# Node stages of a two-layer graph network taken in steps inside the edge passes, with the passes run from the last destinations down

## The chip, the cores and the metric

One core of one Trainium2 chip runs one program. The metric is the device time in microseconds, the median of several executions; lower is better. A core has five engines with instruction streams of their own: TensorE (PE; its weight loads are listed as PEld), VectorE (DVE), ScalarE (ACT), GpSimd (POOL) and SyncE (SP). Each takes its instructions in order, and they meet at semaphores. DMAs are issued from SP, ACT or POOL.

## The reference

N = 30000 nodes with 128 features, E = 960000 edges sorted by destination. The destinations are 30000 times the square of a uniform number, so low node numbers have more edges. Layer 0 has two relational convolutions with 32 edge types, layer 1 a gated convolution with 4 edge types:

```python
def _rel_graph_conv(h, basis, coeff, bias, src, dst, etype, norm):
    W = jnp.einsum('rb,bdf->rdf', coeff, basis)
    Hr = jnp.einsum('nd,rdf->nrf', h, W)
    msg = Hr[src, etype] * norm
    agg = jax.ops.segment_sum(msg, dst, num_segments=N)
    return agg + bias

h = relu(layernorm(x))
h1 = relu(_rel_graph_conv(h, basis1, coeff1, bias1, ...))
x = x + _rel_graph_conv(h1, basis2, coeff2, bias2, ...)
h = relu(layernorm(x))
for t in range(4):
    k, q, v = h @ Wk[t] + bk[t], h @ Wq[t] + bq[t], h @ Wv[t] + bv[t]
    msg = where(edge_type == t, sigmoid(k[dst] + q[src]) * v[src], 0.0)
    outs.append(segment_sum(msg, dst) + h @ Ws[t] + b[t])
x = x + mean(outs)
```

Every convolution reads rows of arbitrary source nodes, so its input table must be complete before it starts.

## The kernel before, in words

**State.** One tile `agg` [128 features x 30080 nodes] stays in SBUF. Each edge pass adds into its columns; `x` and the biases are added to it between passes.

**Before the passes.** The edge arrays are rewritten to offsets within windows (`prep`, line 153), a flag chooses between the path for well-spread sorted edges (`sorted_path`, line 275) and a general one, and the first layer norm writes table `h0` (line 223).

**Edge passes.** `edge_pass` (line 285) runs 25 iterations (`NI`) of 100 groups (`NG`); a group is three tiles of 128 edges whose destinations lie in one window of 32 nodes. Groups come in twenties of five (`NS` = 20 steps of `S` = 5, index `s`, with `g` the place in the five), and four stages of 25 groups per iteration set how far engines may run apart (`stage_boundary`, `leave_stage`). The order of all instructions in an iteration is written out by hand (`manual_schedule`): each engine keeps the order of the program's text.

- In passes c1 and c2 (`rel_body`, line 325) POOL gathers three times 128 source rows (`hg`, line 107, called at 391), DVE builds `sb` (one-hot destination times eight coefficients, line 395), PE multiplies `hg` by `sb` into `pa` (line 401), ACT copies it to `ab` (line 405), and once per five groups PE multiplies by the eight bases into `po` (line 364, `bases_out`) and DVE adds five windows into `agg` (line 323). Once per five groups SP loads edge types `er` (line 337), DVE makes a one-hot `oh` (line 344), PE turns it into coefficients `pc` (line 347) and DVE scales them to `ce` (line 356).
- In pass g (`gate_body`, line 431 on) POOL gathers q and v rows (`qv`), SP loads windows of the k table (`kw`) and types (`kb`), PE picks k rows into `pk` (line 455, `keys`), DVE adds q, ACT takes the sigmoid, DVE multiplies by v into `msg`, and PE sums by window (line 465, `sums`).
- The indices `idx` of an iteration's gathers, with `relc` and `nrm`, are loaded by SP in four parts (`loads`, line 306), one stage ahead.

**Stages between.** Three stages stand between or behind the passes, each a plain loop over all nodes; no gather runs in them.

- Middle (lines 514 to 535): relu of `agg`, transposed and stored as table `h1`; `x` loaded, transposed, plus bias, as the new `agg`.
- Node (lines 540 to 560): for each of 235 blocks of 128 nodes transpose, layer norm, transpose back, three products with weights of 512 columns (line 261), tables `ktab` and `qvtab` stored from ACT and SP, and the node's own product added to `agg`.
- Final (lines 565 to 576): `agg` transposed and stored to the output.

Of the kernel before, what the change touches and what calls it, by code (L numbers as in the profile page):

```python
# [9 lines left out]
F32 = mybir.dt.float32  # L10
# [8 lines left out]
P = 128  # L19
# [24 lines left out]
NI = NGR // NG  # L44
EPS = 1e-5
# [18 lines left out]
def kernel(  # L64
    ctx: ExitStack,
    tc: tile.TileContext,
    x: bass.AP,
    src: bass.AP,
# [28 lines left out]
    h1 = nc.dram_tensor("h1", (NP, D), F32, kind="Internal").ap()  # L97
    agg1 = nc.dram_tensor("agg1", (NA, D), F32, kind="Internal").ap()
    agg2 = nc.dram_tensor("agg2", (NA, D), F32, kind="Internal").ap()
    ktab = nc.dram_tensor("ktab", (NP * T, D), F32, kind="Internal").ap()  # L100
    qvtab = nc.dram_tensor("qvtab", (NP * T, 2 * D), F32, kind="Internal").ap()
# [35 lines left out]
    for i, (bas, cof) in enumerate(((basis1, coeff1), (basis2, coeff2))):  # L137
        bt = consts.tile([P, B, D], F32, name=f"basis{i}")
        nc.scalar.dma_start(bt, bas.rearrange("b d f -> d b f"))
        ct = consts.tile([P, 4, B], F32, name=f"coeff{i}")  # L140
        nc.vector.memset(ct, 0.0)
        for q in range(4):
            nc.scalar.dma_start(ct[q * R:(q + 1) * R, q, :], cof)
        basis.append(bt)
        coeff.append(ct)
# [7 lines left out]
    with tc.tile_pool(name="prep", bufs=2) as prep, \  # L153
# [42 lines left out]
        nc.vector.tensor_reduce(nbad, bad, AX.XY, ALU.add)  # L196
        pbad = prep_ps.tile([1, 1], F32, name="pbad")
        nc.tensor.matmul(pbad, lhsT=nbad, rhs=ones[:TP], start=True, stop=True)
        nc.vector.tensor_copy(flag, pbad)
    n_bad = nc.values_load(flag[0:1, 0:1], min_val=0, max_val=2 * CH * TP)  # L200

    def normalised(pool, xt, kn, name):

        st = pool.tile([P, kn, 6], F32, name=f"{name}_st")
        mv = pool.tile([P, kn, 2], F32, name=f"{name}_mv")
# [3 lines left out]
        rs = pool.tile([P, kn], F32, name=f"{name}_rs")  # L209
        nc.scalar.activation(rs, mv[:, :, 1], AF.Sqrt, bias=eps)  # L210
        nc.vector.reciprocal(rs, rs)
        hn = pool.tile([P, kn, D], F32, name=f"{name}_hn")
# [62 lines left out]
    def sorted_path():  # L275
        with ExitStack() as all_:
            state = all_.enter_context(tc.tile_pool(name="state", bufs=1))
            agg = state.tile([P, NP], F32, name="agg")
# [6 lines left out]
            def edge_pass(name, body):  # L285
                with tc.tile_pool(name=f"{name}_io", bufs=NQ) as io, \
                        tc.tile_pool(name=f"{name}", bufs=2) as pool, \
                        tc.tile_pool(name=f"{name}_c", bufs=1, space=PSUM) as cps, \
# [4 lines left out]
                    nc.vector.tensor_copy(ic, icol)  # L293
                    with tc.For_i(0, NI, 1, iteration_sync="staggered") as i:
                        with tc.manual_schedule():
                            body(i, io, pool, ps, iw, ic)
# [28 lines left out]
            def rel_body(table, bas, cof):  # L325
                def body(i, io, pool, ps, iw, ic):
# [8 lines left out]
                    def types(s):  # L335
                        er[s] = pool.tile([P, TQ, TP], I32, name="er", bufs=3)
# [5 lines left out]
                    def onehot(s):  # L342
                        oh[s] = pool.tile([P, TQ, TP], F32, name="oh", bufs=3)
                        nc.vector.tensor_scalar(oh[s], er[s], icol4, None, op0=ALU.is_equal)  # L344
                        pc[s] = ps.tile([TP, TQ, 4, B], F32, name="pc")
# [24 lines left out]
                    for s in range(2):  # L370
                        types(s)
                        onehot(s)
                    coefficients(0)
                    for s in range(NS):
# [12 lines left out]
                        for g in range(S):  # L387
                            t0 = (s % SB * S + g) * G
                            hg = pool.tile([TP, G, D], F32, name="hg", bufs=20)
# [3 lines left out]
                            for j in range(G):  # L393
                                sb = pool.tile([TP, B, W], F32, name="sb", bufs=15)
# [11 lines left out]
                            if g == 0 and s + 2 < NS:  # L406
                                onehot(s + 2)
                            if g == 1 and s:
                                bases_out(s - 1)
                            if g == 2 and s + 1 < NS:  # L410
                                coefficients(s + 1)
                            if g == 3 and s > 1:
                                add_windows(po[s - 2], base[(s - 2) // SB], s - 2)
                            if g == 3 and s % SB == 1:
                                base[k] = bases(i, k, DVE)
                    bases_out(NS - 1)
                    for s in (NS - 2, NS - 1):
                        add_windows(po[s], base[NQ - 1], s)
                return body

            def gate_body(i, io, pool, ps, iw, ic):
# [30 lines left out]
                def keys(n):  # L452
                    pk[n] = ps.tile([TP, G, D], F32, name="pk", bufs=5)
# [21 lines left out]
                keys(1)  # L475
                for n in range(NG):
# [17 lines left out]
                    if n + 2 < NG:  # L494
                        keys(n + 2)
# [8 lines left out]
                    if g == 4 and s % SB == 0:  # L504
                        base[k] = bases(i, k, DVE)
                sums(NG - 2)
                sums(NG - 1)
                add_windows(po[NS - 1], base[NQ - 1], NS - 1)


            edge_pass("c1", rel_body(h0, basis[0], coeff[0]))


            MB = 4
            with tc.tile_pool(name="mid", bufs=3) as mid, \
                    tc.tile_pool(name="mid_ps", bufs=2, space=PSUM) as mps:
                for b0 in range(0, NB, MB):
                    m = min(MB, NB - b0)
                    cs = slice(b0 * P, (b0 + m) * P)
                    rows = slice(b0 * P, (b0 + m) * P)  # L520
                    r = mid.tile([P, MB, P], F32, name="r")
                    nc.scalar.activation(r[:, :m].rearrange("p m n -> p (m n)"), agg[:, cs],
                                         AF.Relu, bias=b1c)
                    xt = mid.tile([P, MB, D], F32, name="xt")
                    nc.sync.dma_start(xt[:, :m], x[rows, :].rearrange("(m p) d -> p m d", p=P))
                    pr = mps.tile([P, MB, D], F32, name="pr")
                    px = mps.tile([P, MB, P], F32, name="px")
                    for k in range(m):
                        nc.tensor.transpose(pr[:, k, :], r[:, k, :], ident)
                        nc.tensor.transpose(px[:, k, :], xt[:, k, :], ident)  # L530
                    h = mid.tile([P, MB, D], F32, name="h")
                    nc.vector.tensor_copy(h[:, :m], pr[:, :m])
                    nc.scalar.dma_start(h1[rows, :].rearrange("(m p) d -> p m d", p=P), h[:, :m])
                    nc.vector.tensor_scalar(agg[:, cs], px[:, :m].rearrange("p m n -> p (m n)"),
                                            b2c, None, op0=ALU.add)

            edge_pass("c2", rel_body(h1, basis[1], coeff[1]))


            with tc.tile_pool(name="nodew", bufs=1) as nodew, \  # L540
                    tc.tile_pool(name="node", bufs=3) as node, \
                    tc.tile_pool(name="node_ps", bufs=1, space=PSUM) as nps:
                wall, ball, wsm = node_weights(nodew)
                b4 = nodew.tile([P, T], F32, name="b4")
                nc.scalar.dma_start(b4, bass.AP(tensor=bs.tensor, offset=bs.offset,
                                                ap=[[1, P], [D, T]]))
                bsc = nodew.tile([P, 1], F32, name="bsc")
                nc.vector.tensor_reduce(bsc, b4, AX.X, ALU.add)
                nc.vector.tensor_scalar(bsc, bsc, 1.0 / T, None, op0=ALU.mult)
                for b in range(NB):  # L550
                    cs = slice(b * P, (b + 1) * P)
                    px = nps.tile([P, 1, D], F32, name="px")
                    nc.tensor.transpose(px[:, 0, :], agg[:, cs], ident)
                    hn = normalised(node, px, 1, "node")
# [246 lines left out]
```

## Time and profile before

| | us |
|---|---|
| median of 3 runs | 29649.91 (29645.66 to 29655.3) |
| profiled execution | 29622.14, its span 29620.4 |
| start to the first gather of c1 | 346.4 |
| pass c1, first to last gather | 9383.5 |
| pass c2, first to last gather | 9385.5 |
| pass g, first to last gather | 9414.1 |
| middle, node and final stage, about | 108, 859, 79 |

Mean granted TensorE clock: 0.698 of full speed. The costliest groups of instructions (columns: line, engine, operation, tiles, count, then busy time and mean ns of one, then idle time before them with what ended most of it):

```profile
L107 POOL DMA_INDIRECT hg<-h,idx x15000 | 14178.1, 945 | 5056.4 <-issue 4382.0
L401 PE MATMUL pa<-sb,hg 128*128 128x256 f32 x30000 | 11034.6, 490 | 3480.1 <-DMA hg<-h,idx 1943.2
L395 DVE SCALAR_TENSOR_TENSOR sb<-cp,relc,ce 128x256 f32<-128x256 f32 x15000 | 6875.1, 482 | 9188.5 <-PE pa L401 9047.6
L107 POOL DMA_INDIRECT qv<-qvtab,qi x7500 | 7090.4, 945 | 3205.6 <-issue 2900.7
...
L261 PE MATMUL pw<-wall,hT 128*128 128x512 f32 x1410 | 672.0, 613 | 77.2 <-ACT hT L255 77.2
```

A float32 product takes two records, so 30000 records of line 401 are 15000 products. "issue" is idle time in which an engine waited for nothing that the profile shows.

### The profile page before, as it was taken

How to read it: one execution, taken by the hardware profiler on the slowest of the kernel's cores; microseconds unless marked ns; L12 is line 12 of the kernel's file. 1: busy time of each engine (PE TensorE's matmuls, PEld its weight loads, DVE VectorE, ACT ScalarE, POOL GpSimd, SP SyncE). 2: the span in 40 equal slices, each digit the busy share in tenths (PEclk: the TensorE clock that was granted, in tenths of full speed). 3: DMA queues.
4: the chain of work that ended last, by engine and by line, in shares of the span. 5: the costliest groups of instructions: out<-in, count | busy, mean ns of one | idle time of the engine just before them, and what ended most of it. 6: DMA issues, size and time to landing. Idle time of an engine off the chain costs nothing. (4 is left out here: it accounts for less than half of the span.)

```text
span 29620.4 us, 314060 instructions
## 1 busy us (share of the span) xinstructions
PE 22804.0 (77%) x87057; PEld 17713.2 (60%) x87057; DVE 13465.8 (45%) x33126; ACT 3440.9 (12%) x8384; POOL 21269.9 (72%) x22512
## 2 busy tenths in 40 slices
PE   4778787888788788888788888797777777777777
PEld 3555555555555555555555555546666666666666
DVE  5444444444444444444444444464444444444444
ACT  1000000000000100000000000031111111111111
POOL 4777777777777677777777777706777777777776
PEclk8777777777777877777777777795555555555555
DMA  4222222222222322222222222255555555555555
GB/s 124 68 68 69 68 69 68 68 69 69 68 68 69 99 68 68 69 68 68 68 68 68 68 68 68 67 216 183 175 177 175 176 175 175 176 176 175 176 176 173
DMA packets 1707179, 3232.92 MB, mean 109 GB/s; under 512 B 540955, under 2 KB 955931, under 8 KB 1705582
## 3 DMA queue, kind: packets, MB, share of 16 engines
q0 software_dynamic: 840000, 1967.52, 24.3%
q1 hardware_dynamic: 787428, 1135.71, 11.1%
q10 hardware_dynamic: 78154, 109.64, 1.0%
q8 instruction: 851, 13.94, 0.2%
q14 instruction: 746, 6.11, 0.1%
HBM read 2968.58 MB, written 242.53 MB: 108 GB/s over the span
## 5 line engine op out<-in xcount | busy, mean ns | idle before, releaser
L107 POOL DMA_INDIRECT hg<-h,idx x15000 | 14178.1, 945 | 5056.4 <-issue 4382.0
L401 PE MATMUL pa<-sb,hg 128*128 128x256 f32 x30000 | 11034.6, 490 | 3480.1 <-DMA hg<-h,idx 1943.2
L395 DVE SCALAR_TENSOR_TENSOR sb<-cp,relc,ce 128x256 f32<-128x256 f32 x15000 | 6875.1, 482 | 9188.5 <-PE pa L401 9047.6
L401 PEld LDWEIGHTS pa<-sb,hg 128*128 128x128 f32 x30000 | 6031.5, 230 | 7440.9 <-issue 2873.4
L107 POOL DMA_INDIRECT qv<-qvtab,qi x7500 | 7090.4, 945 | 3205.6 <-issue 2900.7
L465 PE MATMUL po<-sel,msg 128*128 128x32 f32 x15000 | 3505.8, 390 | 2510.5 <-DVE msg L463 2506.9
L465 PEld LDWEIGHTS po<-sel,msg 128*128 128x128 f32 x15000 | 3385.1, 325 | 2895.3 <-DVE msg L463 2793.5
L455 PE MATMUL pk<-kw,kb 128*128 128x128 f32 x15000 | 3957.8, 437 | 133.1 <-DVE kb L443 117.2
L405 ACT COPY ab<-pa 128x256 f32<-128x256 f32 x5000 | 1860.4, 372 | 16963.3 <-PE pa L401 16888.6
L496 DVE TENSOR_TENSOR pk<-pk,qv 128x384 f32<-128x384 f32 x2500 | 1413.7, 565 | 4974.3 <-DMA qv<-qvtab,qi 4221.5
L455 PEld LDWEIGHTS pk<-kw,kb 128*128 128x128 f32 x15000 | 3416.7, 327 | 135.8 <-issue 135.8
L364 PEld LDWEIGHTS po<-ab,basis 128*128 128x128 f32 x16000 | 3281.4, 259 | 199.9 <-ACT ab L405 49.5
L364 PE MATMUL po<-ab,basis 128*128 128x160 f32 x16000 | 3236.9, 373 | 23.1 <-ACT ab L405 23.1
L497 ACT ACTIVATE pk<-pk 128x384 f32<-128x384 f32 x2500 | 1185.2, 475 | 7917.6 <-DVE pk L496 7917.4
L323 DVE TENSOR_TENSOR agg<-agg,po 128x32 f32 x7500 | 1399.9, 187 | 1324.3 <-PE po L364 1045.7
L347 PEld LDWEIGHTS pc<-coeff,oh 128*128 128x128 f32 x8000 | 1673.4, 292 | 503.8 <-issue 368.8
L347 PE MATMUL pc<-coeff,oh 128*128 128x32 f32 x8000 | 1526.6, 350 | 359.3 <-DVE oh L344 359.3
L463 DVE TENSOR_TENSOR msg<-pk,qv 128x384 f32<-128x384 f32 x2500 | 1367.8, 548 | 0.0
L443 DVE TENSOR_TENSOR kb<-kb,cp 128x1920 f32<-128x1920 f32 x500 | 1072.5, 2145 | 43.6 <-issue 29.6
L261 PE MATMUL pw<-wall,hT 128*128 128x512 f32 x1410 | 672.0, 613 | 77.2 <-ACT hT L255 77.2
L344 DVE TENSOR_SCALAR oh<-er,icol 128x512 f32<-128x512 int32 x1000 | 553.6, 558 | 79.7 <-issue 32.1
L261 PEld LDWEIGHTS pw<-wall,hT 128*128 128x128 f32 x1410 | 250.0, 190 | 359.9 <-issue 170.3
(70 smaller groups left out, 2629.2 us busy)
## 6 DMA issues: line engine op xcount, KB each, us to landing
kb<-kcode SPq DMA_DIRECT2D x500, 960.0 KB, 5.6
er<-in_et_row SPq DMA_DIRECT2D x1000, 256.0 KB
hg<-h,idx POOLq DMA_INDIRECT x15000, 2.5
kw<-ktab SPq DMA_DIRECT2D x2500, 64.0 KB, 4.7
qvtab<-qvt SPq DMA_DIRECT2D x235, 512.0 KB
qv<-qvtab,qi POOLq DMA_INDIRECT x7500, 3.0
ktab<-kt ACTq DMA_DIRECT2D x235, 256.0 KB
xt<-in_x SPq DMA_DIRECT2D x47, 320.0 KB
```

Of the source, the lines that this page charges most:

```text
L107: nc.gpsimd.indirect_dma_start(out=to, out_offset=None, in_=table, in_offset=bass.IndirectOffsetOnAxis(ap=idx, axis=0))
L323: nc.vector.tensor_add(to, to, po[:, g, :])
L347: nc.tensor.matmul(pc[s][:, c].rearrange("p q b -> p (q b)"), lhsT=oh[s][:, c, :], rhs=cof.rearrange("p q b -> p (q b)"), start=True, stop ...
L364: nc.tensor.matmul(po[s].rearrange("p s w -> p (s w)"), lhsT=bas[:, b, :], rhs=ab[s][:, b].rearrange("p s w -> p (s w)"), start=(b == 0), ...
L395: nc.vector.scalar_tensor_tensor(sb, iw[:TP].unsqueeze(1).to_broadcast([TP, B, W]), relc[:, t0 + j:t0 + j + 1], ce[s].rearrange("p q c b - ...
L401: nc.tensor.matmul(pa.rearrange("p b w -> p (b w)"), lhsT=hg[:, j, :], rhs=sb.rearrange("p b w -> p (b w)"), start=(j == 0), stop=(j == G ...
L405: nc.scalar.copy(ab[s][:, :, g, :], pa)
L455: nc.tensor.matmul(pk[n][:, j, :], lhsT=kb[n // S][:, n % S * G + j, :], rhs=kw[n], start=True, stop=True)
L463: nc.vector.tensor_mul(msg, pk[n], qv[n][:, :, 1, :])
L465: nc.tensor.matmul(po[s][:, g, :], lhsT=msg[:, j, :], rhs=sel[s][:, g * G + j, :], start=(j == 0), stop=(j == G - 1))
L496: nc.vector.tensor_add(pk[n], pk[n], qv[n][:, :, 0, :])
L497: nc.scalar.activation(pk[n], pk[n], AF.Sigmoid)
```

## The change: what it does

1. The edge arrays are reordered on the host, so that iteration i handles the i-th part of the edges from the end: destinations from high to low. Within a part the order stays.
2. With squared uniform destinations, the nodes from 30240 - 1200 i up are complete before iteration i. So iteration i also handles 1200 nodes from there (`VB` = 120, `NPI` = 1200, `LAG` = 240) for the stage that follows this pass. `agg`, `h1`, the tables, `x` and the output have 31440 rows for it. Behind the loop the same steps run once more for the last 1440 nodes, without a written order.
3. Each stage becomes a list of small steps with a place: "at group n of this step's period". `beside(n)`, called at the end of each group, issues them. The middle stage runs in c1 in 5 steps per iteration (240 nodes, parts at groups 0, 3, 5 and 7 of 20), the node stage in c2 in 10 steps (120 nodes, parts at groups 3 to 9 of 10), the final stage in g in 5 steps (240 nodes, parts at groups 4, 6 and 8 of 20). Their stores are all issued by SP, and copies out of PSUM that DVE did are partly ACT's.
4. To make room: `hg` has 10 groups instead of 20, `sb` 12 tiles instead of 15, `er` and `oh` 2 instead of 3, `pc` 1 bank instead of 2, `pk` 4 instead of 5. The one-hot of s + 2 moves from g = 0 to g = 3, and `keys` runs one group ahead instead of two. The bases are loaded at each pass's start.
5. A check is added to `prep`: every part's highest first destination must be low enough for the steps; otherwise the general path is taken.

```diff
+                    each, steps = after(npool, nps)
+                    count = NPI // each
+                    run, period = body(npool), NG // count
                     with tc.For_i(0, NI, 1, iteration_sync="staggered") as i:
                         with tc.manual_schedule():
-                            body(i, io, pool, ps, iw, ic)
+                            todo = {}
+                            for u in range(count):
+                                for at, step in steps(i * -NPI + (N + LAG + u * each)):
+                                    todo.setdefault(u * period + at, []).append(step)
+                            def beside(n):
+                                for step in todo.get(n, ()):
+                                    step()
+                            run(i, io, pool, ps, iw, ic, beside)
+                    for at in range(0, NPI + LAG, each):
+                        for _, step in steps(at):
+                            step()
...
-                        pc[s] = ps.tile([TP, TQ, 4, B], F32, name="pc")
+                        pc[s] = ps.tile([TP, TQ, 4, B], F32, name="pc", bufs=1)
...
-                            hg = pool.tile([TP, G, D], F32, name="hg", bufs=20)
+                            hg = pool.tile([TP, G, D], F32, name="hg", bufs=10)
...
-                            if g == 0 and s + 2 < NS:
-                                onehot(s + 2)
...
+                            if g == 3 and s + 2 < NS:
+                                onehot(s + 2)
                             if g == 3 and s > 1:
                                 add_windows(po[s - 2], base[(s - 2) // SB], s - 2)
                             if g == 3 and s % SB == 1:
                                 base[k] = bases(i, k, DVE)
+                            beside(s * S + g)
...
-                    pk[n] = ps.tile([TP, G, D], F32, name="pk", bufs=5)
+                    pk[n] = ps.tile([TP, G, D], F32, name="pk", bufs=4)
...
-                    if n + 2 < NG:
-                        keys(n + 2)
+                    if n + 1 < NG:
+                        keys(n + 1)
...
+            def after_first(pool, ps):
...
+                    def load():
+                        nc.sync.dma_start(xt, pairs(x[rows, :]))
+                    def relu():
+                        nc.scalar.activation(r.rearrange("p m n -> p (m n)"), cols, AF.Relu,
+                                             bias=b1c)
+                    def turn():
+                        for m in range(2):
+                            nc.tensor.transpose(pr[:, m, :], r[:, m, :], ident)
+                            nc.tensor.transpose(px[:, m, :], xt[:, m, :], ident[:VB, :VB])
+                    def store():
+                        nc.scalar.copy(h, pr)
+                        nc.sync.dma_start(pairs(h1[rows, :]), h)
+                        nc.vector.tensor_scalar(cols, px.rearrange("p m n -> p (m n)"), b2c, None,
+                                                op0=ALU.add)
+                    return (0, load), (3, relu), (5, turn), (7, store)
...
+            def after_second(pool, ps):
+                wall, ball, wsm = node_weights(pool)
...
+                    def bank(name, a, b):
+                        got[name] = ps.tile([P, 4 * D], F32, name="bank")[:a, :b]
+                        return got[name]
+                    def copy():
+                        nc.scalar.copy(xs, cols)
+                        nc.tensor.transpose(bank("px", VB, D), xs, ident)
+                    def norm_():
+                        st["hn"] = normalised(pool, got["px"].unsqueeze(1), 1, "node", VB)
+                    def turn():
+                        pt = bank("pt", P, VB)
+                        nc.tensor.transpose(pt, st["hn"][:, 0, :], ident[:VB, :VB])
+                        nc.scalar.activation(hT, pt, AF.Relu)
+                    def weight(a):
+                        def go():
+                            pw = bank("pw", VB, T * D)
+                            nc.tensor.matmul(pw, lhsT=hT,
+                                             rhs=wall[:, a].rearrange("p t f -> p (t f)"),
+                                             start=True, stop=True)
...
+                            if a == 0:
+                                nc.vector.tensor_add(kt, pw, ball[:VB, 0])
+                                nc.sync.dma_start(knode[rows, :], kt.rearrange("p t f -> p (t f)"))
+                            elif a == 1:
+                                nc.scalar.copy(qvt[:, :, 0, :], pw)
+                            else:
+                                nc.vector.tensor_add(qvt[:, :, 1, :], pw, ball[:VB, 2])
+                                nc.sync.dma_start(qvnode[rows, :],
+                                                  qvt.rearrange("p t a f -> p (t a f)"))
+                        return go
+                    def own():
+                        po = bank("po", P, VB)
+                        nc.tensor.matmul(po, lhsT=wsm, rhs=hT, start=True, stop=True)
+                        nc.vector.scalar_tensor_tensor(cols, xs, bsc, po, op0=ALU.add,
+                                                       op1=ALU.add)
+                    return ((3, copy), (4, norm_), (5, turn), (6, weight(0)), (7, weight(1)),
+                            (8, weight(2)), (9, own))
...
+            def after_third(pool, ps):
...
+                    return (4, copy), (6, turn), (8, store)
...
+            edge_pass("c1", rel_body(h0, basis[0], coeff[0]), after_first)
+            edge_pass("c2", rel_body(h1, basis[1], coeff[1]), after_second)
+            edge_pass("g", lambda npool: gate_body, after_third)
...
+    for k in ("src", "dst", "edge_type_32", "edge_type_4", "edge_weight1"):
+        a[k] = edges(a[k])
```

The tiles of a step come from a pool with one buffer each (two for `xt`, `xs` and `o`), and the node step's products all use one PSUM bank, `bank`. In the changed code, `copy`, `norm_`, `turn`, `weight` and `own` each stand one group after the other.

## The prediction

> **What bounds the kernel now.** I read three views: the page for the shape, the stretches for each stage, and the gathers in order of time around one stage boundary and one boundary between loop iterations.
>
> From the page, the span, the engine totals and the granted clock. The reader is to see that the clock digit drops in the third pass, and that POOL is empty only in the slice that holds the node stage:
>
> ```profile
> span 29620.4 us, 314060 instructions
> ...
> POOL 4777777777777677777777777706777777777776
> PEclk8777777777777877777777777795555555555555
> ```
>
> The stretches: first, second and third edge pass, then the middle stage, the node stage and the final stage (columns: stretch, length, busy time with instruction count of PE, PEld, DVE, ACT, POOL, then clock, DMA share, GB/s). The last three rows have a POOL of zero:
>
> ```profile
> 346.00:9730.00 9384.00, 7533.64 (x26979) 5408.13 (x26979) 4139.20 (x10995) 929.80 (x2499) 7086.92 (x7500) 0.77 0.25 68
> 9850.00:19236.00 9386.00, 7580.09 (x26979) 5426.72 (x26979) 4135.29 (x10995) 929.81 (x2499) 7089.59 (x7500) 0.77 0.25 68
> 20118.00:29532.00 9414.00, 6782.56 (x29976) 6395.41 (x29976) 4268.24 (x8486) 1216.81 (x2524) 7089.38 (x7500) 0.51 0.57 176
> 9738.00:9846.00 108.00, 68.80 (x470) 56.37 (x470) 78.09 (x120) 41.84 (x59) 0.00 (x0) 0.94 0.98 285
> 19246.00:20105.00 859.00, 773.09 (x2342) 378.68 (x2342) 590.09 (x1648) 271.01 (x704) 0.00 (x0) 0.99 0.54 217
> 29541.00:29620.00 79.00, 45.07 (x235) 32.70 (x235) 40.59 (x60) 0.00 (x0) 0.00 (x0) 0.78 0.72 197
> ```
>
> POOL in order of time at the end of the first pass (start, length, idle before):
>
> ```profile
> 9728.66 0.94 POOL L107 DMA_INDIRECT hg<-h,idx  x1 [0.30 <-issue]
> 9729.91 0.94 POOL L107 DMA_INDIRECT hg<-h,idx  x1 [0.30 <-issue]
> 9850.28 0.94 POOL L107 DMA_INDIRECT hg<-h,idx  x1 [119.43 <-DMA idx<-in_src]
> ```
>
> and across an iteration boundary of the second pass; the first gather of the new iteration is that at 10977.16:
>
> ```profile
> 10975.91 0.94 POOL L107 DMA_INDIRECT hg<-h,idx  x1 [0.30 <-issue]
> 10977.16 0.94 POOL L107 DMA_INDIRECT hg<-h,idx  x1 [0.30 <-issue]
> ```
>
> A gather starts every 1.249 us (0.945 busy and 0.30 between two) and does not pause at the boundary. 7500 x 1.249 = 9367 us, against 9386 for a pass: all three passes are bound by POOL's issue of gathers, whatever PE at 77-81% suggests. Between gathers lie only the stages: from last to first gather 120.4 us (9729.9 to 9850.3) and 882.0 us (19235.75 to 20117.73), and 88.6 us from the last gather to the end. That is 1091 us, 3.7% of the span, with POOL idle.
>
> **What the Trainium skill says.** "DMA: Bandwidth & Descriptors", section "SWDGE vs HWDGE vs iDMA": a gather's descriptors are computed by software on GpSimd. The trace agrees: POOL is busy 0.945 us per gather. "SBUF — State Buffer", section "SBUF: two separate sides": some VectorE operations, those with two SBUF inputs or in a two-port mode, can lock GpSimd out. The added VectorE work reads PSUM nearly throughout, and no slowing shows before (gathers last 945 ns in every pass), so I take nothing for it. "TensorE: Matmul & The Clock Gate", Part 1: PE's clock is halved unless recent activity releases it. The trace agrees: see the pairs below. "ScalarE: Activation LUTs", section "Table sets": relu and copy are in every set, so Sqrt in the second pass needs no reload each iteration; before, Copy, Relu and Sqrt ran through two passes and two stages on one load.
>
> **The change part by part.**
>
> *1. Stages removed.* The 1091 us go; what comes back is the drain after each last gather, the few leftover steps behind each loop, and the start of the next pass.
> - First to second pass: drain 8.3 us as now (9729.9 to 9738.2). Six steps of 240 nodes with one buffer for h: each waits for the store before it, copy 0.4 + issue 0.4 + landing 2.4 = 3.2 us (the middle stage shows h waiting on its store 1.3 us with three buffers), plus first load and last landing: 25. The weights now load here: 11.5 us as in the node stage (19246.5 to 19258). Start of pass 5 (9845 to 9850). Sum 50 for 120.4.
> - Second to third: drain 12; twelve steps of 120 nodes, all in one PSUM bank, so one strict chain. By the rows of the node stage: transposes 0.27 + 0.27, statistics 0.29 + 0.18, root 0.30, reciprocal 0.15, normalise 0.41, relu 0.28, three weight products 0.95 each (672.0 us / 705), additions 0.69 x 2, copy 0.59, own product 0.38, addition 0.34: 7.7 us, and some 15 hand-overs of 0.1: 9.4 us. If PE falls to half its clock the products are 1.83 each (six records in 5.49 us at 19255.73): 12.0 us. I take 10.8, so 130 us. Start of the third pass 12, as now (20105 to 20117.7). Sum 154 for 882.
> - End: drain 10, six steps of some 1.8 us, last store: 27 for 88.6.
>
> Together 231 for 1091: 860 us gone.
>
> *2. Steps inside the first and third pass.* Five steps per iteration of 375 us. First pass: four transposes (1.2 us of PE), 0.9 of ACT, 0.45 of DVE each. Third: two transposes and two copies. POOL gets none of it, and the trace has PE waiting for gathers. Cost 0; if the cover failed, 5 x 1.2 us x 25 = 150 us. SyncE takes the stores, the last after group 87 or 88 of 100; 12 groups x 3.75 us remain before the next iteration's indices are needed.
>
> *3. Steps inside the second pass, compute.* Ten per iteration, one per 37.5 us. PE gets 3.8 us each, DVE 2.8, ACT 1.4. DVE now waits four times for PE's product or ACT's root, with the next sb queued behind it and PE behind that: bubbles I estimate at 2.0 + 1.4 + 1.4 + 1.0 = 5.8 us from the same rows. PE's own work per ten groups is 31.6 us (11034.6 + 3236.9 + 1526.6 over 500). Sum 41.2 of 37.5, which would be too much, but the 31.6 is at a mixed clock. When PE has a backlog it runs faster:
>
> ```profile
> 10977.25 0.67 PE L401 MATMUL pa<-sb,hg 128*128 128x256 f32 x2 [0.43 <-DMA hg<-h,idx]
> ...
> 10987.09 2.86 PE L401 MATMUL pa<-sb,hg 128*128 128x256 f32 x6
> ...
> 10990.97 2.40 PE L401 MATMUL pa<-sb,hg 128*128 128x256 f32 x10
> ```
>
> 0.95 us a pair at the lower clock, 0.48 at the higher; thirty pairs then take 14.4 and not 22. Pairing gathers with matmuls in order, PE is 12 us behind at an iteration's start and 4 us behind 19 us later. So PE keeps up, cost 0, up to 925 us (3.7 x 250) if it does not.
>
> *4. SyncE's order in the second pass.* The last step issues its stores at groups 96 and 98, from SyncE; the qvtab store waits for VectorE's addition. The next iteration's idx load stands behind it. Now that load is issued 52 us ahead of its first gather:
>
> ```profile
> 10924.92 0.33 SPq L306 DMA_DIRECT2D idx<-in_src  x1
> ```
>
> After: with group 98's first gather at 0, its data are consumed by about 6 us; at group 96 the bases product (2.4), pw (0.95), addition (0.69) and sb have put PE 3 us back, and pw of group 98 ends near 8.8, the addition near 9.7, the store's issue 10.3, loop end and registers 1.5, idx issued 11.8, gather 2.7 later (9847.6 to 9850.3): 14.5. POOL wanted it at 7.5. A stop of 7 us, bounds 0 (if PE and DVE run well ahead) and 15 (if the steps' backlog is larger); I take 7.5: 24 x 7.5 = 180 us.
>
> *5. Smaller buffers and moved types.* hg 20 to 10 groups: 37 us of lead, PE is at most 14 us behind. One pk less with keys one group earlier instead of two, one pc, fewer er, oh, sb: each still freed a group or more before it is needed. 0; if hg bound, the backlog beyond 37 us would stop POOL, which part 3 prices. Memset 1 us longer, basis load no longer at the start, an added check: 0 within 5.
>
> Sum: 29620 - 860 + 180 = 28940 for the profiled execution. The median of the runs, 29649.9, is 29.5 above the span: **28970**.
>
> **The rivals.**
> - *A, forecast*, 28970.
> - *B, no stop at the boundaries*: SyncE gets to idx in time. For it: PE and DVE have little queued near the end, since no one-hot is made for the last two fives of groups. Against: two groups are left, 7.5 us, less than store issue, loop end and landing alone after a 6 us gather. 28790.
> - *C, a larger stop*: PE's backlog at group 98 is 8 us more, and the leftover chain runs at the half clock: 28970 + 24 x 7.5 + 25 = 29175. For it: PE's clock is 0.77 here. Against: PE catches up between steps.
> - *D, slower*: the second pass becomes PE-bound through the four DVE waits at the mixed clock. 41.2 us per ten groups: 28790 + 925 = 29715, against 29650. It decides from 40.9 us on (860 / 250 = 3.4 us above 37.5). For it: the sum above. Against: the 0.48 us pairs.
> - *E, it does not do what it says*: the added check sends the run down the other path, or the steps fail to lie beside the edges. For the check, destinations are 30000 u squared, so iteration i's lie below 30000 (1 - i/25)^2, always under its limit of 30208 - 1200 i. Then far above 30000.
>
> **How the numbers follow.** A 0.58, B 0.14, C 0.20, D 0.06, E 0.02. Time 28970. The range reaches B's value less 10 for the leftover chains, and C's: 28780 to 29180, which leaves out D, E and the ends. A measurement of this kernel cannot tell less than about 0.2% from no change. Faster by over that: A, B, C, 0.92; slower 0.07; same 0.01 for a D that stops halfway.
>
> **What would show it.** Gather interval 1.25 us in all passes (parts 2, 3, 5); 24 gaps of 5 to 10 us on POOL in the second pass, ended by idx (part 4, and B or C by their length); from last to first gather some 50 and 154 us, 27 at the end (part 1). Wrong if POOL waits for PE's pa in the second pass (D), or if gaps show in the first or third pass too.

## The result, and the profile after

The changed kernel takes 29264.1 us (median of 4 runs, 29255.0 to 29270.5), the kernel before 29647.8 beside it: ratio 0.987, 95% interval 0.9853 to 0.9888. It is faster, by 384 us where 680 were forecast, and the time lies 84 us above the range. The profiled execution is one of the four; its span is 29253.0 us.

The page of the changed kernel, span, POOL's slices and the granted clock:

```profile
span 29253.0 us, 319437 instructions
...
POOL 4777777777777677777777777757777777777777
...
PEclk9888888888888888888888888875555555555555
```

The empty slice is gone (0 became 5), and the clock in the first two passes is higher than before, not lower. The stretches of the changed kernel, the three passes from first to last gather and then what lies behind each (columns as before: stretch, length, busy time with instruction count of PE, PEld, DVE, ACT, POOL, then clock, DMA share, GB/s):

```profile
335.50:9759.70 9424.20, 7087.20 (x27478) 5092.53 (x27478) 4062.63 (x11120) 1014.05 (x2748) 7096.55 (x7500) 0.82 0.26 71
9807.30:19554.00 9746.70, 7150.62 (x29468) 5255.63 (x29469) 4388.45 (x12732) 1216.05 (x3497) 7097.38 (x7500) 0.87 0.32 85
19722.20:29226.50 9504.30, 6810.52 (x30226) 6421.93 (x30226) 4256.11 (x8486) 1299.83 (x2774) 7099.02 (x7500) 0.51 0.56 176
9760.00:9807.00 47.00, 13.72 (x47) 8.79 (x46) 6.79 (x20) 5.84 (x14) 0.61 (x1) 0.54 0.33 88
19555.00:19722.00 167.00, 100.30 (x150) 31.53 (x148) 37.77 (x101) 17.96 (x51) 0.00 (x0) 0.53 0.21 58
```

The stages went as planned, but all three passes grew. Taking the first and last gather of each pass from the trace (us):

| | before | after | difference | forecast |
|---|---|---|---|---|
| start to first gather | 346.4 | 335.5 | -11 | 0 |
| first pass | 9383.5 | 9424.2 | +41 | 0 |
| to the second pass | 120.4 | 47.6 | -73 | -70 |
| second pass | 9385.5 | 9746.7 | +361 | +180 |
| to the third pass | 882.0 | 168.2 | -714 | -728 |
| third pass | 9414.1 | 9504.3 | +90 | 0 |
| last gather to the end | 88.5 | 26.6 | -62 | -62 |
| sum | | | -367 | -680 |

The missing 313 us are 312 in the passes beyond the one stop that was forecast, 11 or 12 in the stages, and 11 the other way at the start. The stop itself is there, in all 24 places. POOL and then SyncE of the changed kernel in order of time at one iteration boundary of the second pass (start, length, idle before and what ended it):

```profile
14086.56 0.94 POOL L112 DMA_INDIRECT hg<-h,idx  x1 [0.30 <-issue]
14087.81 0.95 POOL L112 DMA_INDIRECT hg<-h,idx  x1 [0.31 <-issue]
14096.46 0.94 POOL L112 DMA_INDIRECT hg<-h,idx  x1 [7.71 <-DMA idx<-in_src]
```

```profile
14084.42 0.33 SPq L630 DMA_DIRECT2D ktab<-kt  x1
14090.28 0.33 SPq L635 DMA_DIRECT2D qvtab<-qvt  x1
14092.15 0.38 SPq L340 DMA_DIRECT2D idx<-in_src  x1
```

idx leaves 1.9 us after the qvtab store ahead of it, and POOL stands for 7.7 us instead of 0.3. The 24 stops sum to 166 us (180 forecast). The rest is inside the iterations. Which wait it is, POOL's waits tell (columns: what POOL was to do, what it waited for, us in total, times, longest); before, and then after:

```profile
POOL hg L107 <- DMA hg<-h,idx: 388.9, 1228, 1.2
POOL qv L107 <- DMA qv<-qvtab,qi: 150.8, 373, 2.0
...
POOL hg L107 <- PE pa L401: 77.7, 255, 0.3
```

```profile
POOL hg L112 <- DMA hg<-h,idx: 664.2, 1529, 2.3
POOL qv L112 <- DMA qv<-qvtab,qi: 237.1, 482, 2.6
...
POOL hg L112 <- PE pa L441: 214.3, 669, 1.3
```

POOL is ordinarily idle for 0.3 us between two gathers; a wait costs what it has beyond that. Waits for PE cost 214.3 - 669 x 0.3 = 14 us, so PE is not the bound. Waits for an earlier gather's *landing* (its data are in place and its semaphore says so) cost 664.2 - 1529 x 0.3 = 206 us in the first two passes together, against 21 before; in the third pass 92 against 39. The semaphores named in the trace tell which landing: in the first three quarters of an iteration five semaphores take turns, and a gather waits for the one that the gather five before it completes on. One that has not landed after five intervals, 6.24 us, stops POOL. (In the last quarter eight take turns; more on that below.) What delays the landing shows in SyncE's order inside an iteration of the second pass:

```profile
13737.92 0.39 SPq L630 DMA_DIRECT2D ktab<-kt  x1
13744.67 0.36 SPq L635 DMA_DIRECT2D qvtab<-qvt  x1
13745.53 1.41 SPq L376 DMA_DIRECT2D er<-in_et_row  x2
```

SyncE stood before the qvtab store until VectorE had made its data (SyncE's waits in the whole run, columns as above):

```profile
SPq L635 <- DVE qvt L634: 1631.5, 262, 8.7
```

Two er loads of 256 KB stood behind that store. All three leave within 2.3 us: 480 + 512 KB. Of the 250 qvtab stores of the loop in this pass, 150 have two er loads within 3 us behind them and 27 have one. POOL some 7 us later:

```profile
13749.60 0.94 POOL L112 DMA_INDIRECT hg<-h,idx  x1 [0.30 <-issue]
13751.83 0.95 POOL L112 DMA_INDIRECT hg<-h,idx  x1 [1.28 <-DMA hg<-h,idx]
13753.08 0.94 POOL L112 DMA_INDIRECT hg<-h,idx  x1 [0.30 <-issue]
13755.42 0.94 POOL L112 DMA_INDIRECT hg<-h,idx  x1 [1.39 <-issue]
```

Nine tenths of what is lost between the second pass's gathers falls 6 to 12 us after a qvtab store was issued. In the first pass a waiting h store does the same (4141.42 h, then two er at 4142.29 in the trace): 29 of its 53 us fall 6 to 12 us after one. In the third pass it is the out store with kb and some kw behind it: 65 of its 119 us fall 8 to 12 us after one.

### The profile page after: what moved, and what is told of

The parts are those of the page before. It is cut to its first block, busy times and chain, and to the rows that moved or that the text cites. A ratio compares the mean times of both kernels' runs of the same rounds, so it can differ in the third digit from the quotient of the medians.

```text
span 29253.0 us, 319437 instructions
## 1 busy us (share of the span) xinstructions
PE 21173.6 (72%) x87408; PEld 16818.4 (57%) x87408; DVE 12964.4 (44%) x33272; ACT 3610.0 (12%) x9193; POOL 21297.2 (73%) x22513
## 3 DMA queue, kind: packets, MB, share of 16 engines
q14 instruction: 858, 7.02, 0.1%
## 5 line engine op out<-in xcount | busy, mean ns | idle before, releaser
L441 PE MATMUL pa<-sb,hg 128*128 128x256 f32 x30000 | 9992.9, 462 | 4620.4 <-DMA hg<-h,idx 2150.9
L441 PEld LDWEIGHTS pa<-sb,hg 128*128 128x128 f32 x30000 | 5916.0, 221 | 8230.8 <-issue 3923.4
L435 DVE SCALAR_TENSOR_TENSOR sb<-cp,relc,ce 128x256 f32<-128x256 f32 x15000 | 6373.1, 477 | 3110.7 <-PE pa L441 2527.6
L403 PEld LDWEIGHTS po<-ab,bas 128*128 128x128 f32 x16000 | 2872.4, 231 | 145.0 <-ACT ab L445 37.2
L403 PE MATMUL po<-ab,bas 128*128 128x160 f32 x16000 | 2872.1, 343 | 17.7 <-ACT ab L445 17.7
L386 PEld LDWEIGHTS pc<-coeff,oh 128*128 128x128 f32 x8000 | 1178.5, 214 | 570.3 <-issue 486.0
L386 PE MATMUL pc<-coeff,oh 128*128 128x32 f32 x8000 | 1110.9, 286 | 496.9 <-DVE oh L383 496.9
L629 DVE TENSOR_TENSOR kt<-bank,ball 120x512 f32<-120x512 f32 x262 | 181.2, 692 | 1792.7 <-PE bank L624 1792.7
L624 PE MATMUL bank<-wall,hT 128*120 128x512 f32 x1572 | 857.4, 628 | 23.1 <-DVE kt L629 9.4
L581 DVE TENSOR_SCALAR agg<-both,b2c 128x240 f32 (+1 forms) x131 | 61.2, 467 | 1782.6 <-ACT h L579 1782.6
```

The lines of the kernel that those rows point to most:

```text
L386: nc.tensor.matmul(pc[s][:, c].rearrange("p q b -> p (q b)"), lhsT=oh[s][:, c, :], rhs=cof.rearrange("p q b -> p (q b)"), start=True, stop ...
L403: nc.tensor.matmul(po[s].rearrange("p s w -> p (s w)"), lhsT=bas[:, b, :], rhs=ab[s][:, b].rearrange("p s w -> p (s w)"), start=(b == 0), ...
L435: nc.vector.scalar_tensor_tensor(sb, iw[:TP].unsqueeze(1).to_broadcast([TP, B, W]), relc[:, t0 + j:t0 + j + 1], ce[s].rearrange("p q c b - ...
L441: nc.tensor.matmul(pa.rearrange("p b w -> p (b w)"), lhsT=hg[:, j, :], rhs=sb.rearrange("p b w -> p (b w)"), start=(j == 0), stop=(j == G ...
```

## The experiments

Three theories of the loss within the iterations:
- **Burst.** A store that waits on SyncE holds back the loads queued behind it; store and loads leave together, gathers land late, POOL stops.
- **Volume.** The added bytes cost the gathers the same whenever and from wherever they are sent.
- **Buffers.** hg of 10 groups, one pk less with keys one group ahead and the other smaller buffers, priced at 0 in part 5, stop POOL.

One measure is used throughout: the loss within iterations, the sum over a pass of what the gathers' intervals have beyond the pass's ordinary interval (counted from 0.06 us on). Some of the expectations below give other counts of the same losses (195, 150 and 45 us for the changed kernel; 15, 20 and 47 for the kernel before); the table holds. All from the trace, us; one profiled execution each:

| kernel | first pass | second | its 24 stops | third | ordinary interval | median, all runs |
|---|---|---|---|---|---|---|
| before | 22 | 24 | 0 | 39 | 1.2484, third 1.2501 | 29648 |
| after | 53 | 209 | 166 | 119 | 1.2497, 1.2516 | 29264 |
| after, again | 61 | 209 | 165 | 136 | 1.2484, 1.2501 | 29249 |
| second pass's stores on ScalarE | 54 | 23 | 0 | 141 | 1.2485, 1.2501 | 28904 |
| er on ScalarE | 59 | 67 | 171 | 132 | 1.2485, 1.2501 | 29113 |
| burst rebuilt on ScalarE | 57 | 221 | 0 | 126 | 1.2510, 1.2532 | 29143 |
| all stores apart | 40 | 24 | 0 | 106 | 1.2510, 1.2532 | 28850 |
| before, small buffers | 38 | 38 | 0 | 78 | 1.2484, 1.2502 | 29684 |
| kb on ScalarE too | 43 | 26 | 0 | 154 | 1.2506, 1.2527 | 28913 |
| no out in the loop | 56 | 26 | 0 | 103 | 1.2485, 1.2500 | 28860 |

The kernel before took 29623 to 29648 us beside all of these. The medians of er on ScalarE, burst rebuilt, before with small buffers, and no out in the loop rest on one execution each. How far the loss varies by itself can be read where several kernels have the same code for a pass: 53 to 61 us in the first, 23 to 26 in the second with the stores on ScalarE, 119 to 141 in the third.

**1. The second pass's stores on ScalarE.** The same bytes, the same work, the same buffers; the step starts two groups earlier and its stores leave from ScalarE's queue, which meets them after their data are made:

```
-                                nc.sync.dma_start(knode[rows, :], kt.rearrange("p t f -> p (t f)"))
...
-                                nc.sync.dma_start(qvnode[rows, :],
...
-                    return ((3, copy), (4, norm_), (5, turn), (6, weight(0)), (7, weight(1)),
-                            (8, weight(2)), (9, own))
+                    def store_k():
+                        nc.scalar.dma_start(knode[rows, :], kt.rearrange("p t f -> p (t f)"))
+
+                    def store_q():
+                        nc.scalar.dma_start(qvnode[rows, :], qvt.rearrange("p t a f -> p (t a f)"))
+
+                    return ((1, copy), (2, norm_), (3, turn), (4, weight(0)), (5, weight(1)),
+                            (6, weight(2)), (7, own), (7, store_k), (9, store_q))
```

> Both table stores of the second pass's steps are issued by ScalarE, some groups after the data are made, and the step starts two groups earlier; nothing is left out. SyncE then has only loads in this pass. Burst theory (SyncE's waiting stores hold back the er loads behind them; store and loads then leave together, and gathers that land over 6 us late stop POOL): the 24 stops at the iteration boundaries (166 us) go to 0, and the loss within the second pass's iterations falls from some 195 us to under 60; the second pass takes about 9440 us and the whole some 28930 to 28980 (after: 29264). Volume theory (the 720 KB per step cost the gathers the same wherever they are issued): the boundary stops go, the loss within stays at 180 to 200; pass 9580, whole 29100. Buffer theory (hg of 10 groups instead of 20 stops POOL): the same as volume, 29100.

It and the next two were first run together when the kernel before, too, took 35942 us instead of 29648, with every engine idle in stretches that no semaphore explains; why is not known. They gave 35289, 35459 and 35169 us. There POOL waits above all for PE and VectorE, and the losses within the iterations (over 2100 us in the second pass of each) don't tell the theories apart. Only the stops can be compared: 24 where the stores stay on SyncE, none over 2 us in the other two. All three were run again, the first of them beside the changed kernel:

> The changed kernel itself, unaltered, as the point of comparison on the chip of these runs. In the three runs before this one every engine stood idle for stretches that no semaphore explains, in the kernel before as well (35942 us there, 29648 at first), so this run tells whether that belongs to the chip's condition: if the kernel before takes about 29650 again, this one takes about 29260; if it takes about 35940, this one takes 35250 to 35500 and its trace shows the same idle stretches.

> The kernel with both table stores of the second pass on ScalarE again, beside the changed kernel. If the kernel before takes about 29650: burst theory 28930 to 28980 with a loss of under 60 us within the second pass's iterations and no boundary stops, volume and buffer theory 29100 with 180 to 200 us within. If it takes about 35940: 35290, as measured, and only the boundary stops can be compared.

The changed kernel repeated at 29249. With the stores on ScalarE 28904 us, ratio 0.9756 (0.9728 to 0.9784) to the kernel before, 26 us below the lower end of what the burst theory gave. The stops are gone, the loss within the second pass is 23 us as in the kernel before, and the whole pass takes 9385.0 us (before: 9385.5) with all its steps beside it. ScalarE and SyncE of this kernel, in the same iteration as above:

```profile
13595.37 0.34 ACTq L643 DMA_DIRECT2D ktab<-kt  x1
...
13603.38 0.34 ACTq L646 DMA_DIRECT2D qvtab<-qvt  x1
```

```profile
13597.21 0.53 SPq L376 DMA_DIRECT2D er<-in_et_row  x1
```

One er goes by itself, 6 us ahead of the qvtab store. POOL's waits for landings in this kernel:

```profile
POOL hg L112 <- DMA hg<-h,idx: 295.8, 842, 2.0
```

295.8 - 842 x 0.3 = 43 us are left of the 206, 38 of them in the first pass, which is as it was. Volume and buffers fall for the second pass: neither was changed. The reordered edges fall with them.

**2. Only er moved.** The stores stay where the change has them; `types_on` is `nc.scalar` for the second pass:

```
-                        nc.sync.dma_start(
+                        types_on.dma_start(
                             er[s].rearrange("p c e -> p (c e)"),
```

> The run with only the er loads of the second pass moved from SyncE to ScalarE, again, where the kernel before takes about 29630. Burst theory: the loss within the second pass's iterations falls from 206 us to under 60 (with the stores on ScalarE it fell to 20), the boundary stops stay at 6 to 8 us each; whole 29050 to 29110. Volume and buffer theory, already weakened by the run with the stores on ScalarE: no change, about 29250.

29113 us. The loss within falls to 67 and the time to 3 us above the range, both slightly above what was expected, and the stops stay (171 us), for idx is still behind the last store. This separates the two losses: one has er behind a store, the other idx. Store and er were not parted wholly: 175 of 250 qvtab stores still have one er within 3 us behind them, none has two.

**3. The burst rebuilt, with nothing waiting on SyncE.** As 1, with both er of ten groups behind the qvtab store on ScalarE:

```
+                            if burst and s % 2 == 1 and g == 4 and s + 4 < NS:
+                                types(s + 3)
+                                types(s + 4)
```

> The run with both er loads of ten groups put directly behind the qvtab store on ScalarE, again. Burst theory: 28904 of the run with the stores on ScalarE plus 100 to 190 us within the second pass's iterations, no boundary stops; 29000 to 29090. If it was SyncE's lateness and not the transfers leaving together: 28904 within 20.

ScalarE's queue in this kernel, and POOL behind it:

```profile
13705.65 0.34 ACTq L652 DMA_DIRECT2D qvtab<-qvt  x1
13706.17 1.84 ACTq L376 DMA_DIRECT2D er<-in_et_row  x2
```

```profile
13710.61 0.94 POOL L112 DMA_INDIRECT hg<-h,idx  x1 [0.30 <-issue]
13711.99 0.94 POOL L112 DMA_INDIRECT hg<-h,idx  x1 [0.43 <-DMA hg<-h,idx]
13713.60 0.94 POOL L112 DMA_INDIRECT hg<-h,idx  x1 [0.67 <-issue]
13715.33 0.94 POOL L112 DMA_INDIRECT hg<-h,idx  x1 [0.80 <-DMA hg<-h,idx]
```

No stops, and 221 us within the pass instead of 23: the loss is back in full, from another queue and with er early enough. It is the leaving together that costs, not SyncE. (Whether the store or the two er loads alone would do it was not tried.) The time, 29143, is some 50 above the expected range; 198 are the burst, and the ordinary interval of this execution is 0.0025 to 0.003 us longer, which makes 60 over 22500 gathers. The Trainium skill, "DMA: Bandwidth & Descriptors", section "Issuing engines are not separate DMA queues", says that DMAs interleave on the same 16 engines whichever engine issued them. These runs agree: the burst costs 185 us from SyncE and 198 from ScalarE. What the issuing engine decided here is *when* they leave.

The landings themselves, from the completion counts in the trace, in the second pass (time from a gather's issue to its landing):

| | median | 99 of 100 within | over 5.5 us, of 7500 |
|---|---|---|---|
| before | 2.51 | 6.06 | 253 |
| after | 2.53 | 7.02 | 1016 |
| stores on ScalarE | 2.57 | 5.61 | 108 |
| er on ScalarE | 2.56 | 6.06 | 242 |
| burst rebuilt | 2.57 | 7.00 | 1110 |

That a late landing costs only through the wait for the gather five before shows in the last quarter of each iteration. There the semaphores in the trace take turns in eights instead of fives, so a gather may take eight intervals, 10 us, and the longest of the second pass in these kernels took 7.8. The 1875 gathers of each quarter:

| second pass | quarter 1 | 2 | 3 | 4 |
|---|---|---|---|---|
| semaphores that take turns | 5 | 5 | 5 | 8 |
| after: landings over 5.5 us | 357 | 231 | 288 | 140 |
| after: us lost | 91 | 52 | 65 | 1 |
| burst rebuilt: landings over 5.5 us | 251 | 238 | 344 | 277 |
| burst rebuilt: us lost | 63 | 63 | 91 | 3 |

In the last quarter many landings are late too (in burst rebuilt as many as elsewhere), and next to nothing is lost. In the third pass of the changed kernel it is the same: 149 late landings in the last quarter, 0.0 us lost. More semaphores in the other quarters were not tried.

**4. The other two passes.** As 1, and SyncE issues the h store of the first pass and the out store of the third six groups later in its order:

```
-                    return (0, load), (3, relu), (5, turn), (7, store)
+                    return (0, load), (3, relu), (5, turn), (7, store), (13, out_h)
...
-                    return (4, copy), (6, turn), (8, store)
+                    return (4, copy), (6, turn), (8, store), (14, out_o)
```

> The kernel with the second pass's stores on ScalarE; in addition SyncE issues the first pass's h store six groups later in its order (13 instead of 7) and the third pass's out store six groups later (14 instead of 8), where the data have long been made, so that no load stands behind a waiting store, and out comes behind the last kw of its burst. Nothing is left out. Burst theory: the loss within the third pass's iterations falls from 150 us to 60 to 90 (47 in the kernel before), that of the first from 45 to 15 to 25; whole 28790 to 28850. Volume theory for these two passes, or buffers: 28904 within 15.

28850 us, ratio 0.9737 (0.9721 to 0.9753) to the kernel before: the fastest of all, 1.4% under the changed kernel. (Its profiled execution was the longest of its four, 28909, with the longer ordinary interval; the other three lie within 28847 to 28852.) The first pass's loss falls by 14 us to 40, the third's by 35 to 106. Both are left higher than expected (15 to 25, and 60 to 90), so something else is in these two passes.

**5. The kernel before with the change's buffers alone:** hg 20 to 10, sb 15 to 12, er and oh 3 to 2, pc 2 to 1, pk 5 to 4, and

```
-                    if n + 2 < NG:
-                        keys(n + 2)
+                    if n + 1 < NG:
+                        keys(n + 1)
```

> The kernel before, with nothing of the change but its buffers: hg 10, sb 12, er 2, oh 2, pc 1, pk 4 and keys one group ahead instead of two. Nothing is left out. Burst theory: 29630 within 15, losses within the iterations as in the kernel before (15, 20 and 47 us). Buffer theory: of the third pass's added loss (some 95 us) the part behind no store, 15 to 60 us, appears here, in the third pass alone; whole 29645 to 29690.

29684 us in one execution, 56 over the kernel before in the same runs (29616 to 29638). The third pass loses 39 us more, the first 16 and the second 14, where nothing was expected. In the third pass only pk and keys differ. With keys a group later, kb's buffer comes free later, and kb is issued some three gathers later in its five groups. Nearly all of the pass's loss falls 6 to 10 us after a kb load in both kernels (39 of 39 us, 75 of 78). But kb and five kw leave within 3.0 us (median) in both, and as many gathers of the first three quarters land later than 6.24 us (53 and 54), so why the loss doubles is not shown. Which of the buffers costs the 15 us in each of the other passes was not tried. In the second pass of run 1, with the same small buffers, the 14 us do not appear (23 us).

**6. No out stores in the loop**, on the kernel of 1:

> The kernel with the second pass's stores on ScalarE, with the out stores of the third pass's steps left out in the loop (copies and transposes stay; only the leftover steps write out), so those rows stay unwritten. If the third pass's added loss is the out store with the loads held behind it, on top of later keys: the loss within its iterations falls from 141 us to that of the kernel before with the small buffers, 78 within 15, and the time from 28900 to about 28840. If it is all the buffers, or the steps' own work: 125 to 141 as before, 28900.

28860 us in one execution; the third pass loses 103 us, between the two expectations. From 39 to 141 it goes in three steps: smaller buffers 39, copies and transposes of the steps (and the reordered edges, not tried apart) 25, out with the loads held behind it 37. The third pass of five kernels in which it is the same code lost 119 to 141, and 141 is that of run 1, so the last term may be as low as 16; run 4 took back 35 by moving the out store.

**7. kb on ScalarE**, on the kernel of 4, so that kw need not stand behind a waiting kb:

> The kernel with all stores apart, and in the third pass the kb load issued by ScalarE instead of SyncE, so that the five kw loads no longer stand behind a kb that waits for its buffer, and the out store three groups later still (17). Nothing is left out. Burst theory: kw, kb and out no longer leave together; the loss within the third pass's iterations falls from 106 us to 20 to 60, the time from 28848 to 28770 to 28810. Volume theory for this pass (960 KB of kb and 320 KB of kw in every five groups cost the gathers the same whenever they go): no change, 28848 within 15.

A miss: 28913 us, 63 slower, and 154 us lost instead of under 60. The trace shows two things. At the start of each of the 25 iterations ScalarE now issues two kb together, 1920 KB, where the kernel of 4 issued them at least 11 us apart, and POOL stops some 8 us later:

```profile
23199.27 0.94 ACTq L472 DMA_DIRECT2D kb<-kcode  x2
```

```profile
23207.41 0.95 POOL L112 DMA_INDIRECT qv<-qvtab,qi  x1 [1.74 <-issue]
```

That gather, the tenth of an iteration, has 49 of the 154 us, and none in the kernel of 4. So the move made a larger burst. The other 105 us are the 106 of the kernel of 4, though the fifth kw after a kb now leaves 17 us behind it instead of 3.0 (median): spreading kw brought nothing. The loss still falls 6 to 10 us after each kb (153 of 154 us), so kb alone, 960 KB at once, seems enough of a burst. Sending kb in pieces was not tried.

## Why the prediction was right and wrong

*Part 1, the stages: right, in part by luck.* 48, 168 and 27 us are left for 50, 154 and 27. The 14 us too little are the choice between full and half clock in the chain of twelve steps: a step took 12.6 us (issues of qvtab at 19588.06 and 19600.68) where 10.8 were taken and 12.0 were given for half clock, and the granted clock in that stretch is 0.53. Drain and start took some 17 us for 24. In the 48 us two errors cancel: the six steps took 17 us for 25, the weights and the start of the pass 21.5 for 16.5. (Two slips bear on nothing: the rows show PE at 72% in the third pass, not 77; 7.7 us and 15 hand-overs of 0.1 make 9.2, not 9.4.)

*Part 3, PE and VectorE beside the edges: right.* PE keeps up. The clock rose from 0.77 to 0.87 in the second pass, as the part said of a PE with a backlog (with the smaller buffers alone, run 5, it is already 0.82), and with the stores out of the way the pass takes 9385.0 us, which leaves nothing for the steps' compute. Rival D never came near.

*Part 4, the stop at the boundary: right in place, cause and size,* 6.9 us each for 7.5. Rivals B and C were thereby wrong. The size has some luck in it: counted from group 98's first gather, the qvtab store is issued after 8.4 us for 10.3 and idx after 10.3 for 11.8, but from idx to its gather it takes 4.1 us for 2.7 (means of the 24).

*Part 2 failed:* "POOL gets none of it ... Cost 0". It looked at SyncE's queue at one place, where the next iteration's indices are needed ("12 groups x 3.75 us remain"), and at the engines' time, but at no store within the iteration. 31 us more are lost in the first pass and 80 in the third, plus 10 in each for a longer ordinary interval in this one execution, which the repeated run doesn't have. Of the 31 and 80, 16 and 39 also appear with the smaller buffers alone (part 5). Moving the stores later in SyncE's order took back 14 and 35. Gaps in the first or third pass were a sign of being wrong that the prediction itself had named.

*Part 4 failed in what it left out:* it named the idx load behind the last store, and not the er loads behind each of the other stores, which is the same queue and the same wait. They were 209 - 24 = 185 us of the second pass's 361, more than the 166 of the stop that it did price (10 are the longer ordinary interval). Runs 1 to 3 show it: remove the wait and 23 are left; rebuild the burst elsewhere and 221 are back.

*Part 5 failed:* 0 for the smaller buffers, which cost 69 us over the three passes of the kernel before in run 5. It asked only whether each buffer was freed before it was needed. How they cost it stays open; in the third pass the loss follows the kb loads, which leave later.

These losses (31, 80 and 185 us, part 5's share among them) are 296 of the missing 313 us. Parts 2 and 4 share one omission: they asked whether POOL would find its operands, and took a gather's landing for constant. The profile before had the warning: in the second pass one gather in a hundred landed later than 6 us, when POOL stops at 6.24.

## What to carry to other kernels

When an engine issues its DMAs in order, price every store added to its queue by what stands behind it: a store that waits delays those loads, and lets them go together with it. Issue a store from a queue that meets it when the data are ready, or later in the order; here that was worth 400 us of 29250 (29249 to 28850), as much as the change itself had gained. And before counting a pass bound by the issue of gathers as insensitive, see how late its landings already are against the wait that each issue carries: here the same late landings cost 218 us in three quarters of an iteration, where a gather waits for the one five before it, and 3 us in the quarter where it waits for the one eight before it (run 3).

## What was not expected of the hardware

- 992 KB leaving within 2.3 us stretch the landing of some 64 KB gathers from 2.5 to over 6 us (578 of 7500 in the second pass, 90 before), at a mean DMA share of only 0.32.
- The ordinary interval between gathers differs between executions, the code of the pass being the same: 1.2484 to 1.2510 us (third pass 1.2501 to 1.2532), about 20 us a pass.
- PE's granted clock over the second pass was 0.77 before, 0.82 with the smaller buffers alone, 0.87 with the steps' work as well, and 0.90 with the stores on ScalarE. Work added to PE did not slow its clock; why the buffers alone raised it was not looked into.
